# A Mamba block and a mixture of experts in one kernel: first loads in order of use, q and k side by side, dense products in waits, a last group of three tiles and one, transfers in pairs

## The chip, the cores and the metric

The kernel runs on one core of a Trainium2 chip. It is one launch. The metric is device time in microseconds; every number of a stage is from one profiled execution, and its clock is the clock that the hardware's throttle granted to the matrix engine (1.00 is full speed). The engines are PE (matrix products), DVE or VectorE, ACT or ScalarE, POOL or GpSimd, and SP or SyncE, which issues most DMA transfers in order.

## The reference

The input is 4 sequences of 1024 tokens with 128 features (T = 4096 tokens).

```
# Mamba block, d_inner 256, 16 states, causal convolution of 4 taps
xb, z  = split(x @ in_proj_w.T);  xb = silu(conv(xb))
dt_in, Bp, Cp = split(xb @ x_proj_w.T)
dt = softplus(dt_in * dt_w + dt_b)
h[t] = exp(dt[t] * A) * h[t-1] + (xb * dt)[t] * Bp[t]          # per channel and state
y = sum_n(h * Cp) + xb * D;  y = layernorm(y) * ln_g + ln_b;  y = (y * silu(z)) @ out_w.T
x = layernorm(x + y)
# causal attention, 16 heads of 8, and a mixture of 16 experts
n = layernorm(x);  q, k, v = n @ q_w, n @ k_w, n @ v_w
hidden = x + softmax(q k^T / sqrt(8), causal) v @ o_w
xt = layernorm(hidden);  logits = xt @ router_w
# each token goes to its two best experts, 512 places per expert,
# in order of token; gates are normalised over the two
xin[e] = tokens of expert e;  eout[e] = gelu(xin[e] @ fc1_w[e] + b) @ fc2_w[e] + b
x = layernorm(x + hidden + 0.8 * sum of the gated expert rows)
```

## The kernel before

Tokens are handled in 32 tiles of 128; a half is 4 tiles (512 tokens, half a sequence). The stages follow each other only in part.

**Prologue (L197 to L249).** From the norms of the columns of the q and k weights the kernel computes a bound on the attention scores. It decides on a branch: with small scores no maximum need be subtracted before the exponential. The profiled execution takes this branch (L1567 on). SyncE issues the loads in program order: seven small vectors, then the padded q and k weights, then an identity matrix.

**Fronts (L264).** `front(b, hfs)` makes, for the halves `hfs` of sequence b, the convolution and input projection with 4 shifted products (pt_x) and Silu (xb), the gate (pt_z, sz), the projection to dt, B and C (pt_proj), then dt by Abs, Exp and Ln, and u = xb * dt. ScalarE issues their stores to DRAM. The first front is of one half, the second of the other half, the others of whole sequences. Each switch of ScalarE between Silu, Exp and Ln comes with a table load.

**Scans (L359).** In each half there are 2 blocks of channels (m) by 4 groups of states (g). A step loads dt and u of its channels, broadcast over partitions (dt_sp, u_sp), and rows of B and C (bt, ct), and does: `begin`, h = u * bt on VectorE (2048 columns, L532) and da = exp(dt * A) on ScalarE (4 x 512); `scan`, four recurrences of 512 on VectorE; `gather`, h * ct on VectorE; `sums`, the sum over states on PE. `row(b)` interleaves three steps. `after_scans` then makes the norm of y, the gate, the output projection, the norm that yields x1, and hands it to attention as generators.

**Attention (L657).** `inputs` makes q, k and v of a half; q and k each are split in three bf16 parts (hi, mid, lo), stored to DRAM in a stacked layout (q_parts, k_parts) and read back as kst and qst. `stream` works through four groups of heads: for each tile of 128 keys the scores (pst, L782), their exponential on ScalarE (pr), and the weighted values (av, L804). In the last half each group is divided by its sums at once (`group_of_last`), and the last group is done as two tiles and two (`halves`). `after_projection` adds the residual, normalises (L177), writes the row that goes to the experts (xrow), and makes the logits (lg) by transposes (pt_x2, shown as pt_x) and a product (pl).

**Routing (L1259).** `send` takes a range of tiles: it finds the best and second expert, counts places by products with a triangle and with ones (pcum, ptot), computes the rows to write to (put), and starts one scatter for each tile and choice on POOL (L127). The first 16 tiles are sent during the late scans, "staged": rows are read back from DRAM (L1295) and each scatter waits for the one before. The ranges are of 16, 8, 4 and 4 tiles.

**Experts (L1447).** They read their tokens (xe), run the two products with Gelu, scatter the results to DRAM (eout), and a last stage adds the two rows of each token.

**What sets the order.** While the scans of sequences 1 to 3 run, `piece()` (L1583) advances the generators in the queues `before`, `after`, `final`, `aside`, `loads` and `sending` between scan steps; a generator that yields USE asks to be taken up first in the next piece. When the scans are over, `pace.first` is set and the rest of attention is paced in the same way. PE and VectorE keep this program order (`manual_schedule`, `pinned`); ScalarE, POOL and SyncE are ordered by a scheduler, except for DMAs marked `keep_in_program_order`.

Of the kernel before, what the change touches and what calls it, by code (L numbers as in the profile page):

```python
# [19 lines left out]
P = 128  # L20
# [4 lines left out]
DI = 256  # L25
# [23 lines left out]
USE = 1  # L49
SCORE_MAX = 40.0  # L50
# [3 lines left out]
def mamba_then_moe_block_kernel(ctx: ExitStack, tc: tile.TileContext, a: dict, out: bass.AP):  # L54
# [48 lines left out]

    def clear_slots(ph):
# [18 lines left out]
    def scatter(dst, rows, src, group, earlier=()):  # L123

        ins = nc.gpsimd.indirect_dma_start(  # L127
            out=dst[:, :], out_offset=bass.IndirectOffsetOnAxis(ap=rows, axis=0), in_=src, in_offset=None
        ).ins
        if group is None:  # L130
            return ins
        if group[1]:
            first = [] if earlier else group[1][:1]
            tc.declare_no_dep(ins, group=group[0], keep=first, reason="rows of a group are all different")
            wait_for(ins, first)
        tc.add_to_no_dep_group(group[0], ins)
        group[1].append(ins)
        return ins
# [17 lines left out]
    def inv_std_steps(pool, var, n, tag):  # L156
# [8 lines left out]
        for _ in range(3):  # L165
            nc.vector.tensor_tensor(t, r, r, ALU.mult)
            nc.vector.tensor_tensor(t, t, ve, ALU.mult)
            nc.vector.tensor_scalar(t, t, -0.5, 1.5, ALU.mult, ALU.add)
            nc.vector.tensor_tensor(r, r, t, ALU.mult)
# [6 lines left out]
    def normalise_in_pieces(pool, src, dst, n, tag):  # L176

        mv = statistics(pool, src, n, tag)
        if pace.first:
            r = inv_std_steps(pool, mv[:, :, 1], n, tag)  # L180
        else:
            r = inv_std(pool, mv[:, :, 1], n, tag)
            yield USE
# [20 lines left out]
    qb_pad = load("qb", [P, GQ], a["q_b_pad"])  # L204
    kb_pad = load("kb", [P, GQ], a["k_b_pad"])
    ln1_w = load_columns("ln1_w", a["ln1_w"], 1)
    ln1_b = load_columns("ln1_b", a["ln1_b"], 1)
    ln2_w = load_columns("ln2_w", a["ln2_w"], 1)
    ln2_b = load_columns("ln2_b", a["ln2_b"], 1)
    head_rows = load("head_rows", [P, HG], a["c_head_rows"])  # L210
    with ExitStack() as ph:
        p1 = ph.enter_context(tc.tile_pool(name="bnd", bufs=1))
        ps = ph.enter_context(tc.tile_pool(name="ps_bnd", bufs=1, space=PSUM))
        wq_pad = load("wq", [P, GQ, P], a["q_w_pad"], p1)
        wk_pad = load("wk", [P, GQ, P], a["k_w_pad"], p1)
        pn = ps.tile([P, 2, 2, GQ], F32, tag="pn", name="pn")
        for s, w in enumerate((wq_pad, wk_pad)):
# [3 lines left out]
            for g in range(GQ):  # L221
                nc.tensor.matmul(pn[:, 0, s, g : g + 1], lhsT=sqw[:, g, :], rhs=one_col, start=True, stop=True)
                nc.tensor.matmul(pn[:, 1, s, g : g + 1], lhsT=w[:, g, :], rhs=ln1_b, start=True, stop=True)
# [24 lines left out]
    ident = load("ident", [P, P], a["c_ident"])  # L248
# [15 lines left out]
    def fronts(ph):  # L264
# [8 lines left out]
        w_in = load("w_in", [P, 2 * DI], a["in_proj_wT"], wts)  # L273
        conv_w = f1.tile([P, L], F32, tag="proj", name="conv_w").rearrange("p (d k) -> p d k", k=NTAP)
        nc.sync.dma_start(conv_w, a["conv_w"].unsqueeze(0).to_broadcast([P, DI, NTAP]))
        conv_b = load_columns("conv_b", a["conv_b"], NC2, wts)
# [8 lines left out]
        def front(b, hfs):  # L285
            n, c0 = HL * len(hfs), HL * hfs[0]
            xT = f1.tile([P, L + NTAP - 1], F32, tag="xT", name="xT")
            old = 0 if c0 == 0 else NTAP - 1
            if not old:
                nc.gpsimd.memset(xT[:, 0 : NTAP - 1], 0.0)  # L290
            nc.sync.dma_start(
                xT[:, NTAP - 1 - old : NTAP - 1 + n], a["xT"][:, b * L + c0 - old : b * L + c0 + n]
            )
# [12 lines left out]
            for c in range(NC2):  # L306
                pt = two_banks("pt_z")
                for cols in banks:
                    nc.tensor.matmul(
                        pt[:, cols], lhsT=w_in[:, DI + c * P : DI + (c + 1) * P],  # L310
                        rhs=xT[:, NTAP - 1 + cols.start : NTAP - 1 + cols.stop], start=True, stop=True,
                    )
                nc.scalar.activation(sz[:, c, :], pt[:, :n], AF.Silu)
# [24 lines left out]
            nc.scalar.activation(tmp, tmp, AF.Exp, scale=-1.0)  # L338
            nc.scalar.activation(tmp, tmp, AF.Ln, bias=one_col)
            nc.vector.tensor_tensor(dt, dt, tmp, ALU.add)  # L340
            u = f1.tile([P, NC2, L], F32, tag="tmp", name="u")[:, :, :n]
            nc.vector.tensor_tensor(u, xb, dt, ALU.mult)
            for k, t in (("dt", dt), ("u", u), ("xb", xb), ("sz", sz)):
                for hf, cols in zip(hfs, banks):
                    nc.scalar.dma_start(
                        per_channel[k][b][hf].rearrange("(c p) t -> p c t", p=P), t[:, :, cols]
                    )

# [10 lines left out]
    def scans(ph, pools, on_loads, on_scans, on_half, spare_bank=lambda: None):  # L359
# [41 lines left out]
        def half_of_scans(b, hf):  # L401
# [4 lines left out]

            def spread_states(s, ts, name):
                t = s5.tile([P, HL], F32, tag=name, name=name)
                nc.sync.dma_start(t, bc_d[b][hf][s, len(ts)].unsqueeze(0).to_broadcast([NR, NI, HL]))
# [3 lines left out]
            for m in range(NC2):  # L413
# [4 lines left out]
                for jl in range(NJ):  # L418
                    ch = (NJ * m + jl) * NR
                    for k, t in (("dt", dt), ("u", u)):  # L420
                        nc.sync.dma_start(
# [3 lines left out]
                if m == 0:  # L425
# [4 lines left out]
                    nc.sync.dma_start(y, per_channel["xb"][b][hf].rearrange("(m p) t -> p m t", p=P))  # L430
# [30 lines left out]
        def after_scans(b, hf, y, sz, r):  # L461

            yield
# [3 lines left out]
            for cs in ((0, 1),) if other else ((0,), (1,)):  # L467
# [9 lines left out]
                yield USE  # L477
                for c in cs:
                    nc.vector.scalar_tensor_tensor(
                        sz[:, c, :], pts[c], ln_g[:, c : c + 1], sz[:, c, :], ALU.mult, ALU.mult  # L480
                    )
                for c in cs:
# [1319 lines left out]
```

## Time and profile before

The three runs took 1236.85, 1227.61 and 1236.24 us, median 1236.24. The profiled execution took 1231.79 us, with a span of 1230.0 us from the first instruction to the last and a mean granted clock of 0.845.

| stretch (us) | what runs | PE busy | VectorE busy | clock |
|---|---|---|---|---|
| 0 to 13 | score bound | 3.8 | 2.9 | 1.00 |
| 13 to 62 | first fronts, first loads | 33.4 | 9.7 | 0.95 |
| 62 to 110 | first scans | 37.0 | 45.3 | 0.88 |
| 110 to 860 | scans with attention behind them | 569.9 | 682.3 | 0.83 |
| 860 to 905 | end of the scans, q and k of the last half | 34.9 | 24.3 | 0.94 |
| 905 to 948 | attention of the last half, first group | 35.3 | 20.4 | 0.62 |
| 948 to 1023 | its other groups | 63.1 | 36.5 | 0.89 |
| 1023 to 1062 | last routing, first expert's loads | 13.6 | 16.8 | 0.56 |
| 1062 to 1230 | experts, output | 136.4 | 41.9 | 0.95 |

The busy time of PE has to be read together with the clock: a matrix product at half clock counts as busy for longer. A wait is put down to what came last; idle time of an engine off the path costs nothing.

### The profile page before, as it was taken

How to read it: one execution, taken by the hardware profiler on the slowest of the kernel's cores; microseconds unless marked ns; L12 is line 12 of the kernel's file. 1: busy time of each engine (PE TensorE's matmuls, PEld its weight loads, DVE VectorE, ACT ScalarE, POOL GpSimd, SP SyncE). 2: the span in 40 equal slices, each digit the busy share in tenths (PEclk: the TensorE clock that was granted, in tenths of full speed). 3: DMA queues.
4: the chain of work that ended last, by engine and by line, in shares of the span. 5: the costliest groups of instructions: out<-in, count | busy, mean ns of one | idle time of the engine just before them, and what ended most of it. 6: DMA issues, size and time to landing. Idle time of an engine off the chain costs nothing. (4 is left out here: it accounts for less than half of the span.)

```text
span 1230.0 us, 15488 instructions
## 1 busy us (share of the span) xinstructions
PE 927.4 (75%) x5388; PEld 442.3 (36%) x5388; DVE 880.2 (72%) x1314; ACT 679.0 (55%) x1006; POOL 274.1 (22%) x270
## 2 busy tenths in 40 slices
PE   4787752257889897798988488887778874689975
PEld 2332310033434434324333233323422332466655
DVE  2199698999899999989899998779544546112115
ACT  1567556234787895668875365756443551833324
POOL 1020012130211001100202212553202211244444
PEclk9989976566899998889989687968966995799997
DMA  3965476627464554542563443124654201622117
GB/s 69 304 246 202 158 264 226 215 70 218 134 191 144 162 165 133 159 138 88 170 183 91 146 145 95 54 84 122 153 162 136 73 14 52 171 70 65 48 47 196
DMA packets 170792, 171.03 MB, mean 139 GB/s; under 512 B 32096, under 2 KB 126256, under 8 KB 170576
## 3 DMA queue, kind: packets, MB, share of 16 engines
q1 hardware_dynamic: 155360, 143.16, 38.8%
q10 hardware_dynamic: 11248, 18.35, 4.1%
q0 software_dynamic: 4096, 8.43, 2.1%
q8 instruction: 44, 0.72, 0.2%
q14 instruction: 44, 0.36, 0.1%
HBM read 110.80 MB, written 59.10 MB: 138 GB/s over the span
## 5 line engine op out<-in xcount | busy, mean ns | idle before, releaser
L792 ACT ACTIVATE pr<-pst 128x1024 f32<-128x1024 f32 (+3 forms) x396 | 292.9, 792 | 118.8 <-PE pst L782 67.8
L536 ACT ACTIVATE da<-dt_sp,a_neg 128x512 f32<-128x512 f32 x256 | 179.3, 721 | 124.1 <-DVE h L542 110.0
L782 PE MATMUL pst<-qst,kst 72*128 72x512 bf16 (+3 forms) x792 | 200.1, 356 | 37.6 <-ACT pr L792 18.4
L804 PE MATMUL av<-pr,vp 128*32 128x512 f32 (+3 forms) x1584 | 186.1, 539 | 1.7 <-DVE pr L795 1.6
L532 DVE TENSOR_TENSOR h<-u_sp,bt 128x2048 f32<-128x2048 f32 x64 | 145.4, 2276 | 16.4 <-DMA u_sp<-u_d 16.4
L542 DVE TENSOR_TENSOR_SCAN h<-da,carry,h 128x512 f32<-128x512 f32 x128 | 155.7, 1265 | 1.7 <-ACT da L536 1.7
L542 DVE TENSOR_TENSOR_SCAN h<-da,h 128x512 f32<-128x512 f32 x128 | 148.4, 1205 | 6.7 <-ACT da L536 6.7
L552 PE MATMUL py<-h,sel 128*32 128x512 f32 x512 | 85.0, 743 | 86.6 <-DVE h L548 56.5
L548 DVE TENSOR_TENSOR h<-h,ct 128x2048 f32<-128x2048 f32 x64 | 146.2, 2284 | 1.1 <-POOL carry L545 0.3
L782 PEld LDWEIGHTS <-kst 72*128 72x128 bf16 x792 | 66.5, 103 | 181.9 <-issue 154.9
L545 POOL COPY carry<-h 128x4 f32<-128x4 f32 x32 | 44.5, 1391 | 361.2 <-DVE h L542 342.4
L1477 ACT ACTIVATE hT<-ph,b 128x512 f32<-128x512 f32 x64 | 43.9, 686 | 80.3 <-PE ph L1476 79.3
L127 POOL DMA_INDIRECT eout<-eo,to x64 | 61.3, 957 | 85.0 <-DVE eo L1494 50.4
L301 PE MATMUL pt_x<-xT,w_tap 128*128 128x512 f32 x128 | 63.4, 653 | 18.0 <-DMA xT<-in_xT_dram 8.7
L1476 PE MATMUL ph<-xeT,w 128*128 128x512 f32 x128 | 62.0, 620 | 12.2 <-DVE xeT L1472 12.2
L127 POOL DMA_INDIRECT xin<-row,put x32 | 49.0, 1532 | 75.8 <-issue 31.2
L1490 PEld LDWEIGHTS po_e<-w,hT 128*128 128x128 f32 x496 | 59.7, 192 | 12.7 <-issue 11.9
L788 PE MATMUL pst<-mask_k,identb 128*128 128x128 bf16 x448 | 63.3, 226 | 0.0
L1490 PE MATMUL po_e<-w,hT 128*128 128x128 f32 x496 | 61.3, 277 | 0.0
L127 POOL DMA_INDIRECT xin<-xrow,put x32 | 31.0, 968 | 133.8 <-DMA xin<-xrow,put 46.0
L804 PEld LDWEIGHTS av<-pr,vp 128*32 128x32 f32 x1584 | 36.6, 113 | 61.6 <-issue 38.3
L552 PEld LDWEIGHTS py<-h,sel 128*32 128x32 f32 x512 | 12.4, 118 | 123.1 <-DVE h L548 68.0
(258 smaller groups left out, 1203.6 us busy)
## 6 DMA issues: line engine op xcount, KB each, us to landing
dt_sp<-dt_d SPq DMA_DIRECT2D x64, 256.0 KB
u_sp<-u_d SPq DMA_DIRECT2D x64, 256.0 KB
kst<-k_parts SPq DMA_DIRECT2D x96, 144.0 KB
qst<-q_parts SPq DMA_DIRECT2D x64, 144.0 KB
bt<-bc_d SPq DMA_DIRECT2D x32, 256.0 KB
ct<-bc_d SPq DMA_DIRECT2D x32, 256.0 KB
w<-in_fc_w_dram SPq DMA_DIRECT2D x32, 256.0 KB
xin<-clear SPq DMA_DIRECT2D x8, 516.0 KB
```

The source lines that it names most:

```text
L127: ins = nc.gpsimd.indirect_dma_start(out=dst[:, :], out_offset=bass.IndirectOffsetOnAxis(ap=rows, axis=0), in_=src, in_offset=None).ins
L301: nc.tensor.matmul(pt[:, cols], lhsT=w_tap[:, k, c * P : (c + 1) * P], rhs=xT[:, cols.start + k : cols.stop + k], start=(k == 0), stop=(k ...
L532: nc.vector.tensor_tensor(s.h, s.u, four(s.bt), ALU.mult)
L536: nc.scalar.activation(s.da[jl], s.dt[:, jl, :], AF.Exp, scale=a_neg[:, j, s.g : s.g + 1])
L542: ins = nc.vector.tensor_tensor_scan(h, s.da[jl], h, from_, ALU.mult, ALU.add).ins
L548: nc.vector.tensor_tensor(s.h, s.h, four(s.ct), ALU.mult)
L552: nc.tensor.matmul(s.py[jl * NR : (jl + 1) * NR, :], lhsT=sel, rhs=s.h[:, jl, :], start=(s.g == 0), stop=(s.g == NG_S - 1),)
L782: nc.tensor.matmul(pst[:, jj, :w], lhsT=ks[ki // TPH][jp][:, jj, ki % TPH * P : (ki % TPH + 1) * P], rhs=qs[jp][:, jj, q0:c1], start=True, ...
L788: nc.tensor.matmul(pst[:, jj, :P], lhsT=identb, rhs=mask_k, start=False, stop=True)
L792: nc.scalar.activation(pr[:, :, :w], pst[:, :, :w], AF.Exp, scale=QSCALE)
L804: nc.tensor.matmul(av[32 * j : 32 * j + 32, q0 : q0 + w], lhsT=e.vps[ki // TPH][:, ki % TPH, v0 : v0 + 32], rhs=pr[:, jj, :w], start=(ki = ...
L1490: nc.tensor.matmul(po[:, i, :], lhsT=hT[:, c, i * P : (i + 1) * P], rhs=w2[e][:, c, :], start=(c == 0), stop=(c == NFC - 1),)
```

## The change

Seven things are changed.

1. **First loads.** The padded weights are loaded first in the prologue. In `fronts` conv_w, w_in and xT are loaded before the small weights. In the first front (`alone`) the gate comes last, Exp, Ln, dt, u and their stores are done for each block of 128 channels, and u has a tile of its own. The first loads of the scans keep program order on SyncE, and the first h multiply is four pieces of 512.
2. **Transfers in pairs.** A staged scatter waits for the one before the previous one of its range.
3. **q and k side by side.** When the scans are over, both products come first, in two banks, and the six parts have tiles of their own. `after_scans` starts one piece earlier for the last half, and its squares stand beside the multiplies in opposed order.
4. **Dense products.** `busy(n)` issues n products of the identity with itself, 128 x 128 by 512 columns, whose result nobody reads: 4 ahead of the last half's first scores, 1 and 2 in the normalisation of the last tile, and 1, 0, 1, 0, 6 between the pieces of the last `send`.
5. **Shorter pieces.** The Newton step of the inverse root uses two fused operations for three; the normalisation behind the scans yields ahead of the root and behind it; the residual of the last piece is added later; `soon()` asks for no early turn when the scans are over.
6. **Three tiles and one.** The last group of heads is done for three tiles, then for one; the ranges are of 16, 4, 8, 3 and 1 tiles, and the range of three waits only for the range before (`free`).
7. **Totals.** The product with the totals so far comes first and covers one more column block, so that the new totals come out of it.

Its core:

```diff
+BUSY, BUSY_SUMS, BUSY_NORM = 4, 1, 2
+BUSY_SEND = 1, 0, 1, 0, 6
...
+    def soon():
+        return None if pace.first else USE
...
         for _ in range(3):
             nc.vector.tensor_tensor(t, r, r, ALU.mult)
-            nc.vector.tensor_tensor(t, t, ve, ALU.mult)
-            nc.vector.tensor_scalar(t, t, -0.5, 1.5, ALU.mult, ALU.add)
-            nc.vector.tensor_tensor(r, r, t, ALU.mult)
+            nc.vector.scalar_tensor_tensor(t, t, -0.5, ve, ALU.mult, ALU.mult)
+            nc.vector.scalar_tensor_tensor(r, t, 1.5, r, ALU.add, ALU.mult)
...
         if pace.first:
+            if n > 1:
+                yield
             r = inv_std_steps(pool, mv[:, :, 1], n, tag)
+            if n > 1:
+                yield
...
+            for cs in blocks:
+                nc.scalar.activation(tmp[:, cs, :], tmp[:, cs, :], AF.Exp, scale=-1.0)
+            for cs in blocks:
+                nc.scalar.activation(tmp[:, cs, :], tmp[:, cs, :], AF.Ln, bias=one_col)
+            if alone:
+                u = f1.tile([P, L], F32, tag="proj", name="u").rearrange("p (c t) -> p c t", c=NC2)
+            for cs in blocks:
+                nc.vector.tensor_tensor(dt[:, cs, :], dt[:, cs, :], tmp[:, cs, :], ALU.add)
...
+                store("dt", dt, cs)
+                nc.vector.tensor_tensor(u[:, cs, :], xb[:, cs, :], dt[:, cs, :], ALU.mult)
+                store("u", u, cs)
+            if alone:
+                gate()
...
+            def first_load(t, src):
+                load = nc.sync.dma_start(t, src)
+                if b == hf == m == 0:
+                    tc.keep_in_program_order(load)
...
-            nc.vector.tensor_tensor(s.h, s.u, four(s.bt), ALU.mult)
+            if scan_done:
+                nc.vector.tensor_tensor(s.h, s.u, four(s.bt), ALU.mult)
+            else:
+                for jl in range(NJ):
+                    nc.vector.tensor_tensor(s.h[:, jl, :], s.u[:, jl, :], s.bt, ALU.mult)
...
-            yield
+            if (b, hf) != (B - 1, 1):
+                yield
             sqs = []
...
+            if pace.first:
+                pqs, parts_of = [], []
+                for (n, w, bias), make in zip(sides, (bank, last_bank)):
+                    pqs.append(make("pq"))
+                    nc.tensor.matmul(pqs[-1], lhsT=w, rhs=xnT, start=True, stop=True)
...
+                    nc.scalar.activation(t[0], pq, AF.Identity, bias=bias)
+                    to_parts(n, 0, t[0])
+                yield USE
+                for (n, w, bias), pq, t in zip(sides, pqs, parts_of):
+                    nc.vector.scalar_tensor_tensor(t[3], pq, bias, t[0], ALU.add, ALU.subtract)
+                    nc.scalar.copy(t[1], t[3])
+                    to_parts(n, 1, t[1])
...
-                    halves = 2 if e.last and g == NG - 1 else 1
-                    n = TPH // halves
-                    for i0 in range(0, TPH, n):
+                    if e.last and g == 0:
+                        busy(BUSY)
+                    for i0, n in ((0, TPH - 1), (TPH - 1, 1)) if e.last and g == NG - 1 else ((0, TPH),):
...
+        def busy(n):
+            pst = ps_s.tile([P, 2, HL], F32, tag="ps_s", name="pst_busy")
+            for i in range(n):
+                nc.tensor.matmul(
+                    pst[:, i % 2, :], lhsT=ident, rhs=ident.unsqueeze(1).to_broadcast([P, HL // P, P]),
+                    start=True, stop=True,
+                )
...
             yield
+            if pace.first and not i0:
+                yield
             pt = zbank("pt_x2")
...
-                ins = scatter(xin, s.put[i][:, t : t + 1], row, group, earlier)
-                if group:
-                    wait_for(ins, earlier)
-                else:
-                    in_turn[:] = [ins]
+                before = group[1][-2:-1] if in_turn and len(group[1]) > 1 else earlier
+                scatter(xin, s.put[i][:, t : t + 1], row, group, before)
...
+                before = s.zero if totals[i] is None else totals[i]
+                mms = [(0, n + 1, one_row, before[0:1, :].unsqueeze(1).to_broadcast([1, n + 1, E]))]
+                mms.append((0, n, s.tri, mf))
+                mms += [(t, n + 1, s.ones, mf[:, 0 : (n + 1 - t) * E]) for t in range(1, n + 1)]
...
+                    last = t0 + n > NT - TPH
+                    yield from send(t0, n, bank_z if last else bank, sending.append, free=last)
...
-                for _ in send(early, NT - early, bank):
-                    pass
+                    for i, _ in enumerate(send(early, NT - early, bank)):
+                        busy(BUSY_SEND[i])
```

## Prediction, made before the changed kernel was run

> **What bounds the kernel now.** I read the busy totals first, then the 40 slices, then busy time by stage, and only then the waits and the order in time inside the stages where no engine is full.
>
> ```profile
> PE 927.4 (75%) x5388; PEld 442.3 (36%) x5388; DVE 880.2 (72%) x1314; ACT 679.0 (55%) x1006; POOL 274.1 (22%) x270
> ...
> DVE  2199698999899999989899998779544546112115
> ...
> PEclk9989976566899998889989687968966995799997
> ```
>
> No engine is full over the span, but VectorE is at eight or nine tenths in nearly all of slices 3 to 26. Before that it is nearly idle, behind it PE takes over, and there the granted clock drops to 5 and 6. So there are three places to ask about: the head, the scans, and what follows them. Busy time by stretch (from:to, length, busy us and count of PE, PEld, DVE, ACT, POOL, then granted clock, DMA share, GB/s) says it in numbers:
>
> ```profile
> 13.00:62.00 49.00, 33.35 (x80) 14.44 (x80) 9.73 (x25) 20.03 (x25) 2.45 (x12) 0.95 0.78 229
> 110.00:860.00 750.00, 569.93 (x3499) 243.95 (x3498) 682.26 (x766) 473.54 (x667) 146.57 (x105) 0.83 0.47 149
> 904.00:908.00 4.00, 0.02 (x1) 0.05 (x2) 1.33 (x5) 0.00 (x0) 0.00 (x0) 0.50 0.85 258
> 908.00:916.00 8.00, 7.74 (x36) 2.60 (x37) 2.70 (x12) 4.07 (x5) 0.00 (x0) 0.50 0.73 208
> 924.00:932.00 8.00, 8.00 (x43) 2.41 (x41) 5.03 (x21) 3.55 (x5) 1.70 (x2) 0.50 0.89 270
> 948.00:957.00 9.00, 9.00 (x36) 3.61 (x36) 1.54 (x6) 4.32 (x5) 2.87 (x3) 0.50 0.20 59
> 957.00:1011.00 54.00, 46.28 (x350) 18.72 (x346) 28.69 (x68) 32.48 (x53) 11.73 (x12) 0.99 0.16 47
> 1011.00:1015.00 4.00, 0.45 (x8) 0.00 (x0) 3.38 (x20) 0.84 (x2) 0.00 (x0) 1.00 0.00 0
> ```
>
> From 110 to 860 us VectorE works 682 of 750 us: only the remaining 68 us can be won there. In the head it works 10 of 49. After 904 PE first does nothing for 4 us and then is fully busy at half clock. The waits that end last are these (us in total, times, longest):
>
> ```profile
> DVE h L532 <- DMA u_sp<-u_d: 16.4, 1, 16.4
> ...
> PE pt_x L969 <- DVE xrow L196: 16.4, 4, 4.9
> ...
> PE pst L782 <- DMA qst<-q_parts: 5.2, 1, 5.2
> ```
>
> The same view of SyncE's queue, 745 to 880 us, names what holds back loads during the late scans:
>
> ```profile
> SPq L1295 <- DMA xin<-row,put: 64.6, 13, 8.9
> ```
>
> **Head: -11 us (bounds -6 and -14).** SyncE issues one load per 0.47 us; wq goes eighth, at 4.00 us, and lands at 6.26. First in the queue it saves 3 us of the score bound, which gates the branch. In the branch xT is issued seventh (16.72) and PE starts at 20.22; as third it saves 4 x 0.47 = 1.9 us. So PE starts near 15. Projecting ahead of the gate takes the two pt_z passes (1.1 us) out of the path. Exp (1.06), Ln (1.15), the sum (1.22) and u (1.22) by 128-channel blocks let the first block's stores go about 2 us before the whole would. That puts the first stores near 39 and the last near 42 instead of 44.34 and 45.59. Behind the stores, the broadcast loads of dt and u were issued from 52.2, because SyncE had first issued y, sz_s and eight 256 KB broadcasts, at a DMA share of 0.9. In program order they stand first, with only x, tri and the next xT (1.3 MB, some 4 us at the 315 GB/s of this stretch) ahead. I place the first h multiply at 48 to 50 instead of 62.35. It is now four 512-wide pieces, so a scan need not wait for all 2.28 us. VectorE catches up: g2's multiply, which ended at 83.9, should end about 11 earlier. Against this, the scheduler splits Exp, Ln, Silu of the two fronts so that ScalarE gets six more table loads, three of them between the first da's. In the trace a load takes 1.28 us with nothing around it (Abs ends 38.22, load 38.24, Exp 39.53). [...] By the row they cost 7.7, about 4 of it beside loads that are waited for anyway. I take the row. The low bound, 6, has all of them on the path plus the x loads; the high bound, 14, none.
>
> **Scans: -4 (0 to -8).** Both orders on PE and VectorE are the same here save the pcum products (32 per side become 18, 1 us of PE off the path) and squares beside multiplies. The effect is the pairs: a staged scatter waits for the one before the last. The 32 scatters ran from 748 to 877, 3.3 us apart, SyncE blocked 64.6 us in them; VectorE worked 98 of 125 us in 750 to 875, against 114 at its usual share of 0.91, so some 16 us are lost. Two in flight at most halve that: -8. But the row loads now stand in blocks of 3, 4, 5 and 2 ahead of the kst and q loads on SyncE, and POOL's ssm_rs and lnx_rs behind more scatters at a time; that could give all of it back: 0. I take the middle.
>
> **Behind the scans: -9 (-6 to -11).** From the last lnx_rs (884.3) to the first scores (907.98): on VectorE the earlier half's hid, statistics and 14-operation inv_std ran before q's parts, then q and k ran one after the other (pq 892.87, lo of k 902.98), and qst was issued at 904.41 behind sums and rd, landing 3.57 later. Side by side, with the inv_std after lo_k (12 operations now, the 2 saved are 0.4 us), and one piece less, I get xh, normalisation and statistics to 888, two pq of 0.56 each, hi 0.69 x 2, rest 0.75 x 2, mid and lo 0.65 in turn: lo_k near 894. Six stores of 384 KB (2.25 MB at 300 GB/s = 7.5 us) end near 897 to 898; qst, issued directly behind, lands near 899 to 900. What is late next is these stores.
>
> **The last half: -30 (-12 to -34).** From 907.98 to the last av at 1022.7 it takes 114.7 us in four groups of heads: 34.6, 31.8, 17.7, 30.6. The third ran with the clock at 1.00 throughout. The others lost 4.4 and 3.8 us in waits for xrow (944 to 948, 1011 to 1015), and ran at half clock after each pause: four pst of 512 columns took 1.87 there and 1.03 at full clock, eight av 1.93 and 1.07.
>
> How much the drop costs is disputed. [...] In the trace 28 us of unbroken pst and av (72 rows; 32 columns) stayed at 0.50, to 936; it returned right with the f32 po over 128 x 128 (935.8, again 959.9). So I take the row: dense products restore the clock, scores do not, and one avoided drop in front of group 0 is worth 34.6 - 18 = 17 us. The four products before the first scores last 3.6 us, inside a wait that I estimate at 4 to 5 us after the v products; the idle rest is about 1 us, where a 5.2 us pause lost the clock. The xrow waits go because two yields move pt_x behind more scores (-4.4, -4, plus 9 us at half clock behind the first and 4 behind the last). I sum the groups as 18 + 19 + 17.7 + 18 + 9 for three tiles and one = 82: -33. I give 3 back for product time that no wait covers. If the clock drops anyway: -8 of waits and -4 of half clock, -12.
>
> **Tail: +3 (-2 to +5).** Three tiles and one make two rounds of routing on VectorE in place of one: 38 operations (8.3 us by the 0.2 to 0.3 us of their kinds) for three, then as many for one, against 7.2 from lg (1034.7) to the last put (1042.0). The last puts come near lg + 16.6; but only 2 scatters at 1.27 follow instead of 8, so xe is issued near lg + 19 instead of lg + 15.8 (1050.5). The last products of six keep the clock up, in a wait that hides them; then the experts follow as before.
>
> **Sum.** -11 - 4 - 9 - 30 + 3 = -51. The profiled execution took 1231.8 (span 1230.0); it becomes 1181. The median of the runs shown, 1236.2, is 4.4 above it: 1185.
>
> **Rivals.**
> (a) The clock stays at half for the last half's first group, since the products end too early or are themselves slow: -11 - 4 - 9 - 12 + 5 = -31, so 1205. For it: 1.4 us into the pause at 902.6 the clock was already 0.50. Against: it stayed at 0.95 or more through the shorter gaps of 896 to 904. Chance 0.2.
> (b) The first loads don't move the scans: table loads and x on SyncE eat the head's gain, and the rest holds: 1185 + 9 = 1194. Chance 0.15.
> (c) Slower: the blocks of row loads on SyncE. Each block of up to five rows waits for its scatters; ahead of kst and qst it starves PE's scores, and with PE in fixed order the scans' sums and gathers behind them. At one scatter per 3.3 us five rows hold 33 us. There are four blocks; the other parts bring 47, so from 12 us of lost VectorE time per block the kernel is slower; at 16 it takes 1253. For it: waits of up to 8.9 us exist now. Against: kst is loaded well ahead, and two in flight halve the hold. Chance 0.04.
> (d) No change: products run cold (1.8 us each, 27 in all) and uncovered on top of (a): 1205 + 27 = 1232. Chance 0.03.
> (e) Forecast as above: 0.58.
>
> A measurement of this kernel tells about 1% from no change. Faster by over 1%: 0.93; within: 0.03; slower: 0.04. The range takes in (b) and most of (a), and on the low side head -14, scans -8, tail 0: 1165 to 1208.
>
> **What would show it.** First h multiply near 49; scatters closer than 2 us; first scores of the last half near 900, with PEclk 1.0 in the 15 us behind them; its groups near 18 us each; no wait of pt_x for xrow over 2 us; last put 16 us behind the last lg. The prediction is wrong above all if the clock is 0.5 in that first group, or if VectorE's share in the late scans falls below 0.75.

## The result, and the profile after

The changed kernel takes 1223.28 us (median of 19 runs, 1218.88 to 1227.73), the kernel before 1236.85 (19 runs, 1227.61 to 1248.14). The ratio is 0.9895 with a 95% interval of 0.9873 to 0.9916: about 1% faster, where 4% was forecast. The profiled execution took 1221.69 us with a span of 1219.9, against 1231.79 and 1230.0. The totals and slices of the page of the kernel after, to be laid beside those of before:

```profile
PE 940.2 (77%) x5384; PEld 449.0 (37%) x5384; DVE 883.4 (72%) x1346; ACT 688.0 (56%) x1018; POOL 265.7 (22%) x270
...
DVE  2398698998899998989899998869633467312115
...
PEclk9889976566999998879998778899896987999997
```

They look almost the same. The gain has to be read from points that both programs pass, taken from the two traces in order of time (us):

| point | before | after | its stretch won | forecast |
|---|---|---|---|---|
| first gather of the scans | 73.83 | 69.40 | 4.4 | 11 |
| last gather of the scans | 864.19 | 861.35 | -1.6 | 4 |
| first scores of the last half | 907.98 | 900.03 | 5.1 | 9 |
| last weighted values copied | 1022.71 | 1011.80 | 3.0 | 30 |
| first xe issued | 1050.50 | 1042.12 | -2.5 | -3 |
| end of the span | 1230.0 | 1219.9 | 1.7 | 0 |

The last half holds the error. Busy time by stretch of the kernel after (from:to, length, PE, PEld, VectorE, ScalarE, POOL, then granted clock, DMA share, GB/s) shows what became of it:

```profile
13.00:62.00 49.00, 33.08 (x64) 13.01 (x64) 15.90 (x25) 27.31 (x31) 0.53 (x4) 0.90 0.74 214
110.00:860.00 750.00, 566.82 (x3479) 243.83 (x3481) 679.70 (x767) 470.24 (x664) 147.95 (x110) 0.83 0.47 150
896.00:900.00 4.00, 1.63 (x4) 0.38 (x2) 1.51 (x8) 0.26 (x1) 0.00 (x0) 1.00 0.42 131
916.00:920.00 4.00, 4.00 (x39) 1.60 (x39) 3.19 (x15) 2.82 (x6) 1.15 (x2) 1.00 0.46 154
920.00:924.00 4.00, 0.44 (x6) 0.19 (x4) 3.62 (x20) 0.21 (x1) 1.48 (x2) 0.91 0.70 193
924.00:932.00 8.00, 7.68 (x28) 1.80 (x25) 0.92 (x3) 4.46 (x5) 3.36 (x4) 0.50 0.94 294
932.00:948.00 16.00, 16.00 (x51) 3.00 (x50) 3.77 (x7) 7.33 (x8) 0.00 (x0) 0.50 0.08 23
976.00:980.00 4.00, 0.12 (x2) 0.12 (x2) 3.83 (x8) 0.96 (x2) 0.00 (x0) 0.74 0.00 0
980.00:984.00 4.00, 4.00 (x24) 1.80 (x24) 3.28 (x17) 1.82 (x3) 1.04 (x2) 0.50 0.03 6
```

The clock did hold up in most of the first group (0.90 in the mean of 900 to 924.7, 0.50 from 903 to 906). But at 920 PE stands still again, this time while VectorE is busy for 3.6 of 4 us, and behind that pause come 24 us at half clock. The order in time around it says what VectorE did (start, us, engine, line, operation; some of its instructions left out):

```profile
919.27 0.89 PE L877 MATMUL av<-pr,vp 128*32 128x256 f32 x8
919.39 0.22 DVE L1299 TENSOR_TENSOR loc<-pcum,second 128x64 f32<-128x64 f32 x1
...
921.35 0.16 DVE L1444 SCALAR_TENSOR_TENSOR put<-slot,token 128x4 int32<-128x4 f32 x1
...
921.57 0.55 DVE L945 RECIPROCAL rd<-rd 128x64 f32<-128x64 f32 x1
...
923.24 0.75 DVE L868 TENSOR_TENSOR pr<-pr,tri_f 128x256 f32<-128x256 f32 x2
923.72 0.98 PE L877 MATMUL av<-pr,vp 128*32 128x128 f32 x8 [3.56 <-DVE pr L868]
```

The last key tiles of a group are multiplied by the causal triangle on VectorE before PE weights the values. At half clock, in the kernel before, PE came late enough (its last weighted values of the first group start at 941.76, without a wait); at full clock it arrives while VectorE, in its fixed order, still works off a routing piece and the sums of the half before (919.4 to 923.2). The pause of 3.56 us takes the place of the removed waits. PE's waits from 880 to 1062 us (total, times, longest) confirm that most of those were removed: pt_x waits 4.7 us for xrow, and 16.4 us before.

```profile
PE pcum L1421 <- DVE m L1299: 6.4, 3, 3.9
PE av L877 <- DVE pr L868: 5.0, 4, 3.6
PE pt_x L1056 <- DVE xrow L202: 4.7, 2, 3.3
...
PE pst L855 <- DMA qst<-q_parts: 2.4, 1, 2.4
```

By groups of heads the last half took 24.7, 31.4, 18.9 and 36.8 us, where it had taken 34.6, 31.8, 17.7 and 30.6.

### The profile page after: what moved, and what is told of

It is laid out like the page before. It is cut to its first block, busy times and chain, and to the rows that moved or that the text cites. A ratio compares the mean times of both kernels' runs of the same rounds, so it can differ in the third digit from the quotient of the medians.

```text
span 1219.9 us, 15531 instructions
## 1 busy us (share of the span) xinstructions
PE 940.2 (77%) x5384; PEld 449.0 (37%) x5384; DVE 883.4 (72%) x1346; ACT 688.0 (56%) x1018; POOL 265.7 (22%) x270
## 5 line engine op out<-in xcount | busy, mean ns | idle before, releaser
L855 PE MATMUL pst<-qst,kst 72*128 72x512 bf16 (+3 forms) x796 | 196.6, 348 | 30.1 <-ACT pr L865 19.4
L877 PE MATMUL av<-pr,vp 128*32 128x512 f32 (+3 forms) x1592 | 182.0, 525 | 5.2 <-DVE pr L868 5.0
L591 POOL COPY carry<-h 128x4 f32<-128x4 f32 x32 | 40.1, 1254 | 363.0 <-DVE h L588 329.6
L1563 ACT ACTIVATE hT<-ph,b 128x512 f32<-128x512 f32 x64 | 43.9, 687 | 73.7 <-PE ph L1562 72.9
L861 PEld LDWEIGHTS <-identb 128*128 128x128 bf16 x448 | 43.4, 102 | 26.6 <-issue 7.3
```

The lines of the kernel that those rows point to most:

```text
L855: nc.tensor.matmul(pst[:, jj, :w], lhsT=ks[ki // TPH][jp][:, jj, ki % TPH * P : (ki % TPH + 1) * P], rhs=qs[jp][:, jj, q0:c1], start=True, ...
L861: nc.tensor.matmul(pst[:, jj, :P], lhsT=identb, rhs=mask_k, start=False, stop=True)
L877: nc.tensor.matmul(av[32 * j : 32 * j + 32, q0 : q0 + w], lhsT=e.vps[ki // TPH][:, ki % TPH, v0 : v0 + 32], rhs=pr[:, jj, :w], start=(ki = ...
```

## The experiments

A stage can move by several microseconds between profiles without a change in its program: from the first gather to the 53rd, fourteen profiles with the new head and one order of work there, taken on several chips, took 639.1 to 647.2 us. So stages are compared by the stretch in which kernels differ, and times by ratios to the kernel before on the same chip.

**Four products over the new pause.**

```diff
+                        if e.last and g == 0:
+                            busy(4)
                         for s in before:
                             weighted(*s)
```

> The changed kernel with four more dense products ahead of the last weighted values of the first head group, where PE waited 3.56 us for VectorE's mask multiply at 920 to 924 and then ran at half clock to 949. Theory A (a pause loses the clock, and scores and weighted values do not bring it back): the second group falls from 31.4 to about 20 us, the kernel is 8 to 11 us faster than the changed one, near 1213. Theory B ([...]the half clock had another cause): 0 to 2 us. Theory C (VectorE's routing work is the bound there): the second group keeps its 31 us, and the products cost up to 3.5 us.

The ratio is 0.978 (0.9707 to 0.9854). The second group went from 31.4 to 21.3 us at clock 1.00, as theory A says, and there is no wait there any more. But in this profile the first group lost the clock at 904 and took 30.9 us, so that the two together won only 4. The busy time by head group of this kernel:

```profile
901.20:932.10 30.90, 29.64 (x131) 9.85 (x132) 9.60 (x45) 14.05 (x19) 6.01 (x6) 0.67 0.56 149
932.10:953.40 21.30, 19.42 (x113) 6.37 (x112) 6.47 (x13) 13.99 (x18) 1.91 (x2) 1.00 0.43 130
```

Theories B and C fall: the half clock goes away with the pause (the second group at 0.59 in the changed kernel, at 1.00 here). One half of theory A falls too: in the first group the clock came back at 924, while PE ran scores and weighted values alone.

**Without the first four products.**

```diff
-BUSY, BUSY_SUMS, BUSY_NORM = 4, 1, 2
+BUSY, BUSY_SUMS, BUSY_NORM = 0, 1, 2
...
```

> The changed kernel without the four dense products ahead of the last half's first scores. Theory A: the pause ahead of the first scores (2.4 us then 6 us) loses the clock, and the first group goes back from 24.5 us to about 34; but PE then comes later to the end of the group, where VectorE's routing pieces would no longer be late, so part of it comes back: 3 to 10 us slower than the changed kernel, 1226 to 1233. Rival: the four products are idle ballast, 0 to 3 us faster.

The profile shows what theory A expects: a pause of 4.50 us for qst in place of 2.41, the first group at clock 0.55 in 32.5 us instead of 24.7, the second in 30.4. The time, 0.9882 (0.9808 to 0.9956), does not show the 3 to 10 us of theory A; its interval is wide.

**The old head.** The prologue's loads, the first fronts, the first loads and the first h multiply are those of before.

> The changed kernel with the prologue, the first fronts, the first loads and the first h multiply of before. Theory: the new head wins 4.4 us at the first gather, and VectorE loses nearly all of that again by 490 us, where it waits for PE (pt_yc) at a lower clock; so this kernel is within 2 us of the changed one, 1222 to 1226. Rival: the lead is handed on to the end whenever PE's clock allows, 3 to 5 us slower, 1227 to 1228. The forecast's own figure for the head would make it 11 us slower.

0.9923 (0.9897 to 0.9948) against 0.9895 (0.9873 to 0.9916): the head is worth some 0.3% or 3 to 4 us, and the intervals do not separate that from nothing. The 11 us of the forecast are excluded: they would give 0.998. What the new head does was read in the trace. The first h multiply starts at 49.21 (62.35 before), and those of three steps are done at 62.5. Then VectorE waits for da. ScalarE's order from 56 us:

```profile
56.44 0.57 ACT L342 COPY proj<-pt_proj 128x512 f32<-128x512 f32 x1
...
64.34 1.35 ACT L356 ACTIVATE dt_tmp<-pt_dt,dt_b 128x512 f32<-128x512 f32 x2 [7.34 <-DVE dt L355]
65.59 0.71 ACT L582 ACTIVATE da<-dt_sp,a_neg 128x512 f32<-128x512 f32 x1
66.20 1.04 ACT L366 ACTIVATE dt_tmp<-dt_tmp 128x1024 f32<-128x1024 f32 x1
67.15 0.71 ACT L582 ACTIVATE da<-dt_sp,a_neg 128x512 f32<-128x512 f32 x1
67.87 1.28 ACT L368 ACT_TABLE_LOAD   x1
```

The third and fourth da stand behind Abs of the second front. Abs waited 7.34 us for VectorE's dt, and that had been put behind the multiplies and a scan. So the multiplies came early and the scans did not.

**Transfers in turn.**

```diff
-                before = group[1][-2:-1] if in_turn and len(group[1]) > 1 else earlier
+                before = group[1][-1:] if in_turn and group[1] else earlier
```

> The changed kernel with each staged scatter waiting for the one before, as in the kernel before. Theory: pairs won nothing, since VectorE's wait for POOL and PE behind row blocks took the place of the waits removed: within 1.5 us of the changed kernel, with the last gather near 861. Rival: the pairs are worth 4 us or more, and the last gather comes at 866 or later.

0.9942 (0.9909 to 0.9975) against 0.9895 (0.9873 to 0.9916), so the pairs are worth about 0.5%, though the intervals just overlap: my theory was wrong. That the last gather of this profile came at 858.69, earlier than in the changed kernel, is because this execution had come to the transfers early. From the 53rd gather (some 30 us ahead of the first staged scatter) to the last, the three profiles with transfers in turn took 149.5, 150.1 and 151.1 us, fourteen with pairs 146.7 in the mean (145.1 to 148.1, and one 151.4): 3.5 us, near the 4 of the forecast.

**Only the products, in the kernel before.**

```diff
+                    if e.last and g == 0:
+                        busy(4)
                     halves = 2 if e.last and g == NG - 1 else 1
...
```

> The kernel before, with nothing changed but four dense products ahead of the last half's first scores, where PE waited 5.16 us and the clock fell to 0.50 for 28 us. Theory A (dense products keep the clock and scores cannot bring it back): the first group falls from 34.6 us to 20 to 25, and 5 to 10 us of it reach the end, 1226 to 1231 where the kernel before takes 1236. Rival[...]: the first group stays above 32 us and the time within 2 us. Second rival: VectorE's pieces make PE wait at the end of the now faster group, so that the second group loses the clock instead and under 3 us reach the end.

1.0011 (0.997 to 1.0051): nothing, as the second rival said. The first group fell to 29.2 us, and behind it pt_x waited 4.63 us for xrow: the second group took 36.8 us, 31.8 in the kernel before.

**Three waits covered.** Six products ahead of the first scores, four over the pause at the end of the first group, four ahead of the place count of the eight-tile range:

```diff
+BUSY, BUSY_SUMS, BUSY_NORM = 6, 1, 2
...
+                        if e.last and g == 0:
+                            busy(4)
...
+                if pace.first and n == 2 * TPH and i == 0:
+                    busy(4)
```

> The changed kernel with six dense products ahead of the first scores in place of four, four ahead of the last weighted values of the first group, and four ahead of the second routing range's first place count, where PE waited 3.88 us for VectorE at 976. Theory A: no half clock from the first scores to the start of the last group, the first group near 24 us, the second near 21, the third near 19, together 64 instead of 75: 8 to 12 us faster than the changed kernel, near 1213. Rival: the products only fill time in which VectorE is late, 0 to 3 us.

0.9798 (0.9719 to 0.9878). The groups took 24.8, 23.6, 23.3 and 35.7 us, 107.4 in all; the first three make 71.7, where theory A had 64. The three pauses are gone, and still the clock fell twice in the second and third group. A fine view of the first fall:

```profile
920.00:923.00 3.00, 2.92 (x16) 0.92 (x15) 1.62 (x8) 0.99 (x2) 1.20 (x2) 1.00 0.60 155
923.00:924.00 1.00, 0.33 (x2) 0.19 (x2) 0.00 (x0) 1.00 (x2) 0.83 (x1) 1.00 0.99 331
924.00:925.00 1.00, 0.68 (x4) 0.10 (x1) 0.00 (x0) 1.00 (x2) 0.13 (x1) 0.85 1.12 352
925.00:931.00 6.00, 6.00 (x23) 0.95 (x21) 0.69 (x1) 3.41 (x4) 0.96 (x1) 0.50 0.85 260
```

No long wait stands before it: PE was a third to two thirds busy for two microseconds, while the first exponentials of a group are made. The clock was back after 7 us, at about 931.5, and no product over 128 rows and 128 columns had run since the fall, only scores, weighted values and two bf16 products of 48 rows. The durations show it (four scores of 512 columns, 1.89 us at half clock and 1.04 at full):

```profile
927.85 1.89 PE L855 MATMUL pst<-qst,kst 72*128 72x512 bf16 x4
...
931.86 1.04 PE L855 MATMUL pst<-qst,kst 72*128 72x512 bf16 x4
```

**Group starts filled too.** On top of the edit before:

```diff
                             now = [(ki, jp) + scores(ki, jp, i0 * P, (i0 + n) * P) for jp in range(2)]
+                            if e.last and ki == 0 and i0 == 0:
+                                busy(2)
```

> The kernel with six, four and four covering products, and two more dense products behind the first key tile's scores of every head group of the last half, where PE was busy a third to two thirds for 2 us and the clock fell to 0.50 for 7 and 10 us. Theory A: the clock stays up through the second and third group, each 3 to 4 us shorter, less about 1 us each for the products: first scores to last values 102 to 105 us instead of 107.4. Rival: the products hold the score buffers and cost as much as they win, 107 or more.

Theory A holds in this profile: the granted clock stays at 1.00 from the first scores (902.7) to 992.2 us, and first scores to last values take 104.0 us. The ratio is 0.9787 (0.9722 to 0.9852), not told apart from the edit before. The head groups of this kernel, the last one in its two parts:

```profile
902.70:927.40 24.70, 22.38 (x135) 8.49 (x136) 9.38 (x45) 13.76 (x18) 5.85 (x6) 1.00 0.71 189
927.40:949.20 21.80, 21.05 (x117) 7.04 (x117) 6.46 (x13) 14.11 (x18) 1.92 (x2) 1.00 0.42 127
949.20:969.40 20.20, 19.19 (x117) 6.82 (x118) 9.47 (x37) 14.26 (x19) 0.00 (x0) 1.00 0.17 51
969.40:992.20 22.80, 21.28 (x141) 9.59 (x140) 17.50 (x49) 10.24 (x18) 9.90 (x10) 1.00 0.09 28
992.20:1006.70 14.50, 11.56 (x112) 6.92 (x109) 7.97 (x7) 5.64 (x17) 5.75 (x6) 0.76 0.10 32
```

So this is what the half costs with the clock at 1.00 up to its last part: PE is busy 95.5 of 104 us. By tile, the dense products are 15.1 us of it, and the work of the half before and of routing (po, pr, pcum, pl, transposes) 3.6 us in the first group and 5.9 in the second.

**Two tiles and two.**

```diff
-                    for i0, n in ((0, TPH - 1), (TPH - 1, 1)) if e.last and g == NG - 1 else ((0, TPH),):
+                    for i0, n in ((0, 2), (2, 2)) if e.last and g == NG - 1 else ((0, TPH),):
...
-                            then(group_of_last(e, g, t, rows, i0, n), n if g == NG - 1 else 0, final if i0 else after)
+                            then(group_of_last(e, g, t, rows, i0, n), TPH if i0 + n == TPH and g == NG - 1 else 0, final if i0 else after)
```

> The changed kernel with the last head group in two tiles and two and one last routing range of four, as before. Theory: the last group's 36.8 us (30.6 before) come from the routing of eight tiles that now falls beside it and from half clock, not from the split; so the group stays at 33 to 37, and the tail from the last values to the first xe issue goes from 30.3 back to about 28: within 3 us of the changed kernel. Rival (the split itself costs): last group back to 31 and 5 us faster. Rival (the split is worth what was forecast, 9 us less work in the last piece): 4 us or more slower.

The last group took 33.4 us and the tail 30.8, so the tail did not come back: with two tiles at the end PE waits 4.55 us for their sums. The ratio, 0.9786 (0.9703 to 0.9868), lies below that of the changed kernel, which no reading of this profile explains. It is from four runs on another chip; below, on one chip, the split makes no difference. It speaks against the rival that the split is worth 9 us. It is a warning too: with no product more than the changed kernel, this one has the ratio of the covered ones, so what the covers win can be read only from kernels on one chip.

**The range of eight tiles first.**

```diff
-if not aside and not before and early < known < NT and (early == SOON or known > NT - 2 * TPH):
+if not aside and not before and early < known < NT and known >= SOON + 2 * TPH and (early == SOON or known > NT - 2 * TPH):
```

> The changed kernel with the ranges of tiles routed in the order of the kernel before, eight tiles and then four, by holding the first of these until two halves are done. Theory: VectorE's 8-tile routing leaves the last groups, whose time falls from 36.8 us to 31 to 33, while the mask multiply at the end of the first group still waits about as long (3 to 5 us): 2 to 6 us faster than the changed kernel. Rival: the heavier range beside the first and second group costs there what is won at the end, 0 us.

0.9873 (0.9786 to 0.996), and the last group still took 36.8 us. My theory that the eight tiles make it long falls, but not that routing does: the range of four tiles now stands beside the last group, and PE waits 3.6 us there for its place count, where it waited 3.88 for that of eight. The first group rose to 29.6 us, with a wait of 5.64 us for kst.

**Early turns.**

```diff
     def soon():
-        return None if pace.first else USE
+        return USE
```

> The changed kernel in which the generators ask for early turns behind the scans too, as before. Theory: the half ahead of the last is finished earlier, so that the second routing range no longer stands beside the last head group, and the last group falls from 36.8 us toward the 30.6 of before; the mask multiply of the first group may wait as before: 2 to 6 us faster than the changed kernel. Rival: VectorE then comes late at the other pieces, no change or slower by up to 4 us.

0.9972 (0.9929 to 1.0015): slower than the changed kernel by about 0.8%, and the rival was nearer than my theory. PE waits for the mask multiply six times, 7.7 us in all, and 4.2 us for a place count; the mean granted clock of this profile is 0.835, of the changed kernel's 0.856, and first scores to last values take 124.7 us. So with the rest of the new pacing the early turns cost time; whether the new pacing as a whole wins any is asked below.

**q, then k.**

```diff
-            if pace.first:
+            if False:
...
-            for n, w, bias in () if pace.first else sides:
+            for n, w, bias in sides:
```

> The changed kernel with q and k of the last half one after the other, as in the kernel before. Theory: the first scores come 4 to 8 us later behind the last gather (39.7 us in the changed kernel and its variants), the rest is the same: 4 to 8 us slower than the changed kernel. Rival: the loads are hidden by the half before, whose pieces fill the time: under 2 us.

The first scores come 43.4 us behind the last gather; in the twelve other profiles with q and k side by side and the new pacing it is 38.2 to 40.3. So side by side wins 3 to 5 us at that point. The ratio, 0.9824 (0.9763 to 0.9885), does not show them at the end.

**The pacing of before.** Early turns, the yields in the normalisation and ahead of pt_x taken out, and eight tiles first.

> The changed kernel with the pacing behind the scans of before: early turns, no added yields in the normalisation and ahead of pt_x, the range of eight tiles first. Theory: no mask-multiply wait of 3.6 us at the end of the first group, but the wait of pt_x for xrow (4.4 us) returns behind it, so that the second group still runs at half clock; the last group falls to about 31: 0 to 6 us faster than the changed kernel. Rival: the new pacing is what the change lives on, 3 us or more slower.

0.9845 (0.9785 to 0.9906), not told apart from the changed kernel, so the rival falls: nothing shows that the new pacing as a whole wins time. The mask multiply's pause is gone and pt_x waits 3.51 us for xrow, as expected; kst came late (5.84 us), and the last group, with no routing beside it, took 33.3 us.

**The covered kernel in both splits, and the changed kernel, on one chip.** The first is the kernel with filled group starts, with the last group in two tiles and two.

> The kernel with the six, four, four and two covering products, and the last head group in two tiles and two with one last routing range of four. Theory A: with the clock up, the last group's 37 us of three and one fall to 30 to 32, the tail is the same within 2 us (a range of four in place of three and one): 4 to 7 us faster than the same kernel with three tiles and one. Rival: the last group is bound by VectorE's routing of eight tiles and reciprocals in both splits, under 2 us.

> The kernel with six, four, four and two covering products, again, beside the changed kernel on one chip. Theory A: 8 us less from the first scores to the last values, as in its profile, so 6 to 12 us faster than the changed kernel. Rival: the earlier difference was the chip's, under 4 us.

> The changed kernel itself, for comparison with its covered versions on one chip: 0.987 to 0.992 of the kernel before by the runs so far; 1.0 would say that its gain depends on the chip.

The ratios are 0.9819 (0.9775 to 0.9864), 0.9809 (0.9768 to 0.985) and 0.9895 (0.9851 to 0.9938). Here the medians stand side by side: the covered kernel takes 1221.6 us, the changed one 1231.3 and the kernel before 1242.7. So the covers win about 0.9% or 10 us; the split makes no difference that shows. The covers did not hold the clock throughout this time: in the second profile of the covered kernel it fell at 914 for 7 us, behind a wait of 3.38 us for kst (0.89 in the mean of 900 to 930, 1.00 from 930 to 960). From the first scores to the last values it took 115.5 us, and the changed kernel 120.3. In these profiles the last group took 44.7 us in the covered kernel, 43.9 in two and two, and 44.6 in the changed one. A part of it is a stall of ScalarE, here in the second profile of the changed kernel:

```profile
985.55 1.51 ACT L865 ACTIVATE pr<-pst 128x768 f32<-128x768 f32 x2 [0.98 <-PE pr L988]
991.78 1.51 ACT L865 ACTIVATE pr<-pst 128x768 f32<-128x768 f32 x2 [4.71 <-remote]
```

PE's scores for it were ready before 989, and the trace names no engine or transfer that released it. What it is stays open, and so does how much of the last group's length is due to it: the first profile of the changed kernel and that of the kernel with filled starts have no such stall, and took 36.8 and 37.3 us. Of the seventeen profiles six have one, of 3.6 to 5.2 us, and their last groups took 40.8 to 44.9 us; without it none took over 37.3.

**What carries the gain of 1%.** Taken back singly, the pairs (0.5%) and, less surely, the head (0.3%) show in the time. The kernels without the first products, with q then k, with two and two, or with the pacing of before were not slower than the changed one. The shorter inverse root, the totals and the dense products behind the last group were not tried alone.

## Why the prediction was wrong

It forecast 1185 (1165 to 1208) and the measured median is 1223.28. The step that failed is **the last half, -30**; the head's -11 was mis-sized.

*Last half, -30: it won 3.* Of the 41 us that the profile lacks, 27 are lost here. Half of its mechanism was seen. Behind the pauses of 5.16 and 4.42 us in the kernel before, and of 3.56 us in the changed one, the clock was 0.50; with four products over the last of these the second group ran at 1.00. And a busy PE did not always bring it back: behind the 3.56 us it stayed at 0.50 from 924 to 948, with PE busy for 23.7 of these 24 us. But "dense products restore the clock, scores do not" is too strong. The second of the two returns that it was read from was not at the po: in the trace of before, the scores ahead of po already run at full speed.

```profile
957.94 1.04 PE L782 MATMUL pst<-qst,kst 72*128 72x512 bf16 x4
...
959.90 1.12 PE L907 MATMUL po<-ob_diag,ones_f 128*128 128x512 f32 x2
```

Nor were the 28 us to 936 of scores and values alone: place counts and bf16 products of 48 rows stood among them. What brings the clock back in one place and not in another stays open.

Two things were wrong in the sum. First, 18 + 19 + 17.7 + 18 + 9 = 82 took its group time from the one group that had little other work beside it (2.3 us). With the clock at 1.00 in all but the last part, the covered kernel needs 24.7 + 21.8 + 20.2 + 37.3 = 104: the first groups carry the work of the half before, and 15 us are the products themselves. "3 back for product time" was too little by far with the clock at 1.00 up to 992. Second, the step asked what PE waits for at its old pace. At full clock PE reached the mask multiplies before VectorE did, and the pause of 3.56 us and the half clock behind it gave back what the first group had won: 34.6 to 24.7 in the first, then 31.4 where 19 was forecast. I had listed a new wait as what a rival does, and put it at SyncE, not at VectorE's queue.

*Three tiles and one.* Forecast as 27 us for the group; it took 36.8, and the forecast counted little but scores and values. These took 9.7 and 10.5 us of PE, just as in the kernel before, where the group took 30.6. Sums, output products and place counts brought PE to 28.6 us (23.1 before), and it stood still for 8.2, of which 3.9 were for a place count; in the kernel before no routing stood beside this group. Two and two took 33.4 us in one profile and 0.8 less than three and one in a pair with the stall, so the split explains 3.4 us at the most; how the rest divides stays open. The tail was right, and in its steps: +2.5 against +3, with xe issued 19.4 us behind the first lg, forecast 19.

*Head, -11: 4.4.* The first multiply was right to a microsecond (49.2), in part by luck: PE started at 17.2 and not near 15, as it waited for VectorE's w_tap, and the last store went at 45.6 and not near 42; what won was that the loads of dt and u went ahead, from 43.7. The step that failed is "VectorE catches up": it gave the multiplies their time and let the scans follow, and did not follow ScalarE's order to the third and fourth da. The table loads took 1.28 us each, as the row had said, but what counted was who stood in front of da.

*Scans, -4.* Right in size for the pairs (3.5 us). But the profile's last gather came only 2.8 us earlier, since the lead, still 4.0 us at 415, was 0.9 at 483. There VectorE waited 2.5 us for pt_yc, and the clock from 460 to 470 was 0.66, where it had been 1.00 before. Of the thirteen other profiles with this order, nine were still 2.8 us or more ahead of the same profile of before at about 498, and three under 1. So nothing shows that the change brings this loss; it varies between executions.

*Behind the scans, -9: 5.1 in the profile.* Parts done and stores were as forecast (lo_k 9.6 us behind xh, forecast 9.7). qst was issued at 897.4, not directly behind the stores, as it waited for q_parts to land; from xh to the first scores it took 18.3 us where the sum had 15 to 16.

Of the rivals, (a) came true one group later than it said, (b) in part, and (c) and (d) did not. The chance of 0.93 for faster by over 1% stands beside a result of 1.05%.

## What to carry to other kernels

Before a wait is removed, ask which engine the freed one will meet next, at its new pace: here the matrix engine, faster through the first group (24.7 us for 34.6), ran into the vector queue that had been ahead of it at half clock, and in its pinned order waited there for 3.56 us. Size a stage at full clock by its own list of work, with the neighbours' pieces and the filler in it, not by its best quarter. Put filler where PE would idle, and over all such places of a stretch: here, over its waits and latency gaps, it won 10 us net on one chip (1221.6 against 1231.3); ahead of the first wait alone, in the kernel before, nothing (1.0011). And before a return of the clock is put down to an instruction, look whether the ones ahead of it already run at full speed, as the scores at 957.94 did (1.04 us).

## What the runs showed of the hardware

The clock fell without a long pause too: after two microseconds in which PE was 33% and 68% busy it went to 0.50 (923 to 925 in the kernel with three waits covered). A busy PE brought it back in some places and not in others. In the changed kernel it stayed at 0.50 for 24 us of nearly unbroken work, 72-row bf16 scores and 32-column f32 weighted values with four bf16 products of 48 rows among them, and came back with f32 products over 128 rows and columns (po, from 947; 0.73 from 949 to 952). In the kernel with three waits covered it came back at 931.5, in that with four products over the new pause at 924, and in the kernel before at 957.9, each time with scores and weighted values just ahead of it. With the waits covered and two products in each group's start it stayed at 1.00 for 89 us in one profile (902.7 to 992.2); in a second it fell for 7 us behind a wait of 3.38 us. A dense f32 product of 512 columns showed as two passes of 0.59 us at full clock, and four in a row took 3.70 us (from 893.93 in the changed kernel). Profiles of one order of scans, on several chips, took 639.1 to 647.2 us from the first gather to the 53rd; from 460 to 470 the clock was 0.66 in the changed kernel and 1.00 in the kernel before.
